# Turning image blocks on the vector engine: an edit of the first-image stages of a two-layer kernel

## The chip, the cores and the metric

The kernel runs on one core of a Trainium2 chip. The metric is device time in microseconds of one execution; lower is better. Before the change the median of three runs is 2614.22 us (2608.95 to 2623.82). All data are 32-bit floats.

## The reference, cut to what matters

The reference has two layers over an image of 256 x 256 pixels with 128 channels. The first is gated attention over rows. The second takes the channel axis as width: it sees 256 tokens, each an image of H = 256 by W = 128, and applies Fourier layers. The change touches the mixer at the end of the second layer:

```python
h0 = instance_norm(attn, norm2_w, norm2_b)
h1 = fno_layer(h0, mix_wr[0], mix_wi[0], ..., (H, W), norm=True, act=True)
h2 = fno_layer(h1, mix_wr[1], mix_wi[1], ..., (H, W), norm=True)
out = instance_norm(h2, mon_w, mon_b) + attn
```

Here `fno_layer` is a skip (a 4 x 4 mix of the tokens of a group), plus a spectral convolution that keeps 32 frequencies along H and 16 along W, then, in the first of the two, a gelu. So after the gelu of h1 the kernel needs its Fourier transform: first along w (16 complex frequencies, 32 real rows), then along h. It also needs the statistics of the second skip of h1, for the norm.

## The kernel before, in words

The tokens are worked on in two halves, `a` = 0 and 1, of 128 tokens each. A half is an array of 128 partitions (tokens) by 256 x 128 pixels, cut into 16 blocks of 16 rows h, so 2048 pixels to a block. The half in work lies in SBUF in the tile `blocks`, and `hb[b]` is block b. Of its 16 rows, `by_turn` makes four turns j of four rows each.

The stage in question is `first_images` (L1720 to L1852), which runs once for each half. For each block it does the following.

- `first_skip` (L1813) multiplies the block by the 4 x 4 mixes, as 16 tiles of 32 x 32 of the array, into four PSUM banks `ups`, one for each turn. The banks come from pool `psk`, which has four.
- `image` (L1386) adds the inverse transform of the modes (tile `gs`, loaded from `Gd1`) into the same banks.
- `gelu` (L1819) has ScalarE (ACT) read a bank and write the gelu into `hb[b]`: four instructions.
- `turn_back` (L1770) has TensorE (PE) transpose the 16 pieces of 128 x 128 of a block against the identity into four banks `htps` of pool `pst` (four banks as well). VectorE (DVE) copies them into `hT`, and in half 1 ACT copies the one of turn 0 (L1780, L1789). The copies of turns 1, 2 and 3 also exchange pieces of 32 or 64 tokens, since a turn holds its tokens in exchanged order.
- `along_w` (L1800) multiplies by `bfwd` (128 pixels of w by 32 rows) into one bank `psA`, four tiles of 128 x 32 at once. ACT copies it to `yA`, and GpSimd (POOL) issues the store into `Yd` in HBM (L1808); the very last of half 1 is issued by ACT.
- `second_skip` (L1793) multiplies the block by the mixes of the second layer into four banks `sps` of `pst`, and DVE takes their statistics (`bn_stats`, L1798). Only the statistics are kept.

The order is written out by hand (`manual_schedule`), for the compute engines and for the queue of SyncE (SP), which issues the loads. In pass b of the loop at L1827 the order in half 0 is: first skip of b, second skip of b-2, image of b, gelus 0 and 1, transform of b-2, gelus 2 and 3, turn of b-1. In half 1 the second skip comes first. So PE has transform and turn to do behind an image.

Beside it, half 0 prepares w, the sum that the output needs: `add_w` (L1747) has ACT scale the block (L1755), POOL add x1 (L1758) and issue the store to `wd` (L1759). This is done in halves of a block, for 21 of 32; the other 11 are done earlier. In half 1 the generator `output_0` (L2151) writes out half 0 in between: after the turn of a pass it multiplies a block's second skip and image into four banks `h2ps` of pool `psk` (L2135 to L2137), ACT empties two of them and DVE two (L2139 to L2144), and then DVE adds w twice (L2148) and POOL issues the stores (L2149).

After the stage, `second_modes` (L1882, half 0) or `LastModes` (L1961, half 1) loads `Yd` into `YT` and transforms along h. `ystat` (L1440) holds the statistics of y that `first_modes` (L1653) sums up.

Tiles of one tag rotate through a fixed number of buffers, so an instruction that writes a buffer waits for those that read what was in it. That holds for PSUM banks too: the fifth bank asked of `pst` is the first again.

Of the kernel before, what the change touches and what calls it, by code (L numbers as in the profile page):

```python
# [10 lines left out]
FP = mybir.dt.float32  # L11
# [7 lines left out]
P = 128  # L19
# [681 lines left out]
def layer1(tc, I, C, ident, x1d, upool, U, Q2, groups, out):  # L701
# [6 lines left out]
    nc = tc.nc  # L708
    NT, H, W = 256, 256, 128
    L = lambda n: I["L1_conv_" + n]  # L710
    with ExitStack() as ctx:
# [667 lines left out]
        def by_turn(t):  # L1379

            return t.rearrange("p (n j w) -> p j n w", j=4, w=W)

        def rows_of(ps):
            return ps.rearrange("p (n w) -> p n w", w=W)

# [51 lines left out]

        sp = sp3
        hstat = sp.tile([P, 64, 6], FP, name="hstat")
        ystat = sp.tile([P, 2, 64, 6], FP, name="ystat")  # L1440
# [59 lines left out]
        def y_blocks(a, psum, lo, hi, also=None):  # L1500

            tt = slice(a * P, (a + 1) * P)
            gs = {}

            def load(u):
                if (a, u) not in xts:
                    xts[a, u] = load_x1(a, u)
                if u % 2 == 0:
                    gs[u // 2] = xp.tile([P, 4, P], FP, tag="gs", name=f"gs_{a}_{u}", bufs=3)
                    load_modes(gs[u // 2], Gd0, u // 2, tt)  # L1510

            load(lo)
            load(lo + 1)
            yield 0.0
            for u in range(lo, hi):
                b, s = u // 2, u % 2
                if u + 2 < hi:
                    load(u + 2)
                xt = xts.pop((a, u))
                ps = [psum.pool.tile([P, 512], FP, tag=psum.tag, name=f"yps_{a}_{u}_{j}") for j in range(4)]  # L1520
                ps = [z[:, 0:256] for z in ps]
                for j in range(4):
                    for sc in range(2):
                        nc.tensor.matmul(  # L1524
                            rows_of(ps[j]), mpT[:, sc, tt], by_turn(xt[:, sc])[:, j],
                            start=(sc == 0), stop=False,
                        )
                    if j < 3:
                        yield 0.86
                image(ps, gs[b], bsy, range(2 * s, 2 * s + 2))  # L1530
                if a == 0:
                    yt = blocks[:, b, s * HB : (s + 1) * HB]
                else:
                    yt = xp.tile([P, HB], FP, tag="yt", name=f"yt_{u}")
                for j in range(4):
# [107 lines left out]
        def first_modes(a, wp, mk, psum, gts):  # L1643
# [9 lines left out]
            nc.vector.bn_aggr(h.col[:, 0:2], ystat[:, a].rearrange("p k s -> p (k s)"))  # L1653
# [66 lines left out]
        def first_images(a, wp, yp, psk, pst, first=None, modes=()):  # L1720
# [44 lines left out]
            if a == 0:  # L1765
                load_w(0)
                add_w(0)
            hTs = {}

            def turn_back(b):  # L1770

                turned = by_turn(hb[b])
                hT = hTs[b] = {}
                for j in (1, 2, 3, 0):
                    ps = pst.tile(f"htps_{a}_{b}_{j}")
                    for n in range(4):
                        nc.tensor.transpose(ps[:, n * P : (n + 1) * P], turned[:, j, n, :], ident)  # L1777
                    t = hT[j] = wp.tile([P, 512], FP, tag="hT", name=f"hT_{a}_{b}_{j}", bufs=4)
                    if j == 0:
                        (nc.scalar.copy if a else nc.vector.tensor_copy)(t, ps)  # L1780
                        continue
                    v = t.rearrange("p (n c d x) -> p n c d x", n=4, c=2, d=2)
                    if j == 1:
                        v = v[:, :, :, ::-1].rearrange("p n c d x -> p (n c) d x")
                    elif j == 2:
                        v = t.rearrange("p (n c x) -> p n c x", n=4, c=2)[:, :, ::-1]
                    else:
                        v = t.rearrange("p (n c x) -> p n c x", n=4, c=4)[:, :, ::-1]
                    nc.vector.tensor_copy(  # L1789
                        v, ps.rearrange("p (m c x) -> p m c x", m=v.shape[1], c=v.shape[2])  # L1790
                    )

            def second_skip(b):  # L1793

# [4 lines left out]

            def along_w(b):  # L1800

                hT = hTs.pop(b)
                psA = pst.tile(f"psA_{a}_{b}")
                for j in (1, 2, 3, 0):
                    nc.tensor.matmul(psA[32 * j : 32 * j + 32, :], bfwd, hT[j], start=True, stop=True)  # L1805
                yA = wp.tile([P, 512], FP, tag="yA", name=f"yA_{a}_{b}")
                nc.scalar.copy(yA, psA)
# [74 lines left out]
        def second_modes(a, wp, mk, psum, gts, yts):  # L1882
# [5 lines left out]
            def load(c, hcs=(0, 1)):  # L1888
# [2 lines left out]
                    YT[c] = yp.tile([P, 2, 2, 512], FP, tag=tag, name=f"YT_{a}_{c}", bufs=bufs)  # L1891
                for hc in hcs:
                    nc.sync.dma_start(
                        YT[c][:, hc],
                        h.Yd[P * hc : P * hc + P].rearrange("h (r f) t -> h r (f t)", r=2)[
                            :, :, 4 * c * P : 4 * (c + 1) * P
                        ],
                    )

            def forward(c):  # L1900
                ps = psum.tile(f"f1ps_{a}_{c}")
                for r in range(2):
                    for hc in range(2):
                        for k in range(2):
                            for f in range(4):
                                nc.tensor.matmul(
                                    ps[32 * f : 32 * f + 32, r * P : (r + 1) * P],
                                    efwd[:, hc, (2 if r else 1) if k else 0, :],
                                    YT[c][:, hc, 1 - r if k else r, f * P : (f + 1) * P],
                                    start=(hc == 0 and k == 0), stop=(hc == 1 and k == 1),  # L1910
                                )
                nc.vector.tensor_copy(F[:, c].rearrange("p r t -> p (r t)"), ps[:, 0:256])
# [48 lines left out]
        class LastModes:  # L1961
# [5 lines left out]
            def load(self):  # L1967

                tile = lambda tag, bufs, n, name: xp.tile([P, 2, n], FP, tag=tag, name=name, bufs=bufs)
                rows = halves[1].Yd.rearrange("h (r f) t -> h r (f t)", r=2)  # L1970
                self.low = [tile("xt", 3, 1024, f"YT0_{k}") for k in range(2)]
                for k in range(2):
                    nc.sync.dma_start(self.low[k], rows[0:P, :, 1024 * k : 1024 * k + 1024])
                self.high = [tile("yt", 2, 512, f"YT1_{k}") for k in range(2)] + [tile("xt", 3, 1024, "YT1_2")]
                at = (slice(0, 512), slice(512, 1024), slice(1024, 2048))
                for lo, hi in ((0, 96), (96, P)):
                    for t, c in zip(self.high, at):
                        nc.sync.dma_start(t[lo:hi], rows[P + lo : P + hi, :, c])

            def spectrum(self, c, hc, r, f):  # L1980
                if hc == 0:
                    t, c = self.low[c // 2], c % 2
                else:
                    t, c = self.high[min(c, 2)], c % 2 if c > 1 else 0
                return t[:, r, 512 * c + f * P : 512 * c + (f + 1) * P]

            def synth(self, c, banks, gt, engines):

# [307 lines left out]
def constants():  # L2296
    H, W = 256, 128
    N = H * W
# [159 lines left out]
```

## Time and profile before

| | us |
|---|---|
| median of three runs | 2614.22 |
| profiled execution | 2609.25 |
| its span on the core | 2607.5 |
| first images of half 0, about | 1957 to 2083 |
| first images of half 1, about | 2233 to 2410 |
| PE busy in 1955 to 2083 | 118.74 of 128 |
| PE busy in 2230 to 2410 | 161.80 of 180 |
| DVE busy in the same two | 82.33 and 126.94 |
| ACT busy in the same two | 74.39 and 86.49 |
| POOL busy in the same two | 79.15 and 27.45 |
| transfers in the same two | 269 and 343 GB/s |

The profiled execution took 2609.25 us, of which the span of the core's records is 2607.5; it is 5 us below the median. A line of the timeline has the start in us, the busy time, engine, source line, operation, output and inputs, the shape and, after x, how many instructions were merged; a bracket at its end has the idle time before them and who ended it. A matmul's busy time overlaps that of the next, so that the step from start to start is the better measure. One 32-bit multiplication shows as two matmul instructions.

### The profile page before, as it was taken

What the parts mean: (1) busy time and instruction counts of PE and PEld (TensorE: products, weight loads), DVE (VectorE), ACT (ScalarE), POOL (GpSimd) and SP (SyncE); (2) the same over time, 40 slices, a digit from 0 to 9 for tenths busy, and PEclk for the clock granted to TensorE, in tenths of its full rate; (3) what the DMA queues carried; (4) which work ended last, traced back from release to release, by engine and by line L of the source; (5) the groups of instructions that cost most, each with busy time, mean ns of one, the idle gap of its engine ahead of it and who ended that gap; (6) DMA issues with size and microseconds to landing.
All of it is one profiled execution on the core that took longest, in us unless ns stands there. A gap on an engine that the chain in (4) does not pass through costs nothing. (4 is left out here: it accounts for less than half of the span.)

```text
span 2607.5 us, 88724 instructions
## 1 busy us (share of the span) xinstructions
PE 2393.2 (92%) x37598; PEld 1557.0 (60%) x37598; DVE 2051.0 (79%) x2908; ACT 1399.1 (54%) x2700; POOL 1474.4 (57%) x1043
## 2 busy tenths in 40 slices
PE   7799999999999999999999999998989988799754
PEld 6555656566556565665655667787675566455533
DVE  7799999999999999999998547566656655577455
ACT  0377888888888888888887222100016401344232
POOL 1299999999999999999997003001136511111011
PEclk9999999999999999999999999999999998899855
DMA  9755566666566565565663110788898774999599
GB/s 364 222 101 104 102 108 105 105 107 105 104 108 106 104 106 104 106 107 102 109 105 71 23 59 16 258 274 260 310 336 279 251 242 138 334 365 318 190 382 345
DMA packets 1016549, 458.49 MB, mean 176 GB/s; under 512 B 831062, under 2 KB 946729, under 8 KB 1009752
## 3 DMA queue, kind: packets, MB, share of 16 engines
q1 hardware_dynamic: 980120, 364.71, 55.5%
q0 software_dynamic: 22832, 81.54, 8.1%
q10 hardware_dynamic: 13200, 6.56, 0.9%
q8 instruction: 298, 4.88, 0.8%
q14 instruction: 99, 0.81, 0.1%
HBM read 317.36 MB, written 135.27 MB: 174 GB/s over the span
## 5 line engine op out<-in xcount | busy, mean ns | idle before, releaser
L422 POOL TENSOR_TENSOR e<-e,b1T 128x1024 f32<-128x1024 f32 x255 | 604.5, 2370 | 83.3 <-ACT e L404 82.7
L427 POOL TENSOR_TENSOR es<-e 128x512 f32<-128x512 f32 x512 | 648.0, 1288 | 0.1
L449 DVE RECIPROCAL av<-av 128x256 f32<-128x256 f32 x256 | 452.2, 1766 | 9.1
L404 ACT ACTIVATE sc<-sc,b2T 128x512 f32<-128x512 f32 x514 | 339.9, 662 | 123.1 <-PE sc L395 110.9
L404 ACT ACTIVATE e<-sc,b2T 128x512 f32<-128x512 f32 x510 | 322.9, 693 | 0.0
L420 DVE TENSOR_TENSOR e<-sc,b1T 128x1024 f32<-128x1024 f32 x257 | 312.2, 1215 | 6.7 <-ACT sc L404 3.5
L395 PE MATMUL sc<-qkT 32*128 32x256 f32 x4096 | 294.4, 401 | 1.8 <-DVE e L420 1.8
L437 PE MATMUL av<-e,v 128*32 128x256 f32 x4096 | 268.6, 379 | 1.8 <-DVE gate L450 1.7
L1524 PE MATMUL yps<-xt,mpT 128*128 128x256 f32 x1024 | 246.7, 391 | 22.3 <-DVE yt L1536 15.1
L395 PEld LDWEIGHTS sc<-qkT 32*128 32x128 f32 x4096 | 185.7, 184 | 113.7 <-issue 52.3
L1524 PEld LDWEIGHTS yps<-xt,mpT 128*128 128x128 f32 x1024 | 192.0, 193 | 67.5 <-DVE yt L1536 20.4
L437 PEld LDWEIGHTS av<-e,v 128*32 128x32 f32 x4096 | 130.1, 109 | 125.9 <-issue 38.5
L1540 POOL DMA_DIRECT2D yd<-yt x32 | 17.4, 544 | 320.1 <-DVE yt L1536 315.4
L2149 POOL DMA_DIRECT2D out_dram<-w x64 | 34.2, 534 | 258.9 <-DVE w L2148 258.2
L367 ACT ACTIVATE qkT<-qk,qb 128x512 f32<-128x512 f32 x256 | 174.0, 680 | 3.1 <-PE qk L337 3.0
L337 PE MATMUL qk<-turned,wT_wk 128*32 128x256 f32 x2048 | 163.9, 392 | 0.8 <-DVE g_ve L35 0.8
L494 ACT ACTIVATE turned<-turned 128x256 f32<-128x256 f32 x256 | 104.3, 408 | 112.2 <-DVE x1b L462 109.8
L337 PEld LDWEIGHTS u<-adft,x 128*32 128x32 f32 x4096 | 118.4, 110 | 74.9 <-issue 74.7
L442 PE MATMUL av<-es,ones 128*32 128x256 f32 x2048 | 160.7, 379 | 1.6 <-POOL es L427 1.6
L345 DVE STREAM_TRANSPOSE turned<-xk 128x1024 f32<-128x1024 f32 x128 | 158.1, 1235 | 0.4 <-DMA xk<-in_L_conv_kv_x_dram 0.4
L337 PE MATMUL qk<-turned,wn_wq 128*32 128x256 f32 x2048 | 157.9, 380 | 0.0
L1822 ACT ACTIVATE blocks<-ups,turn 128x512 f32<-128x512 f32 x128 | 92.5, 781 | 89.0 <-PE ups L1391 55.8
(575 smaller groups left out, 4277.1 us busy)
## 6 DMA issues: line engine op xcount, KB each, us to landing
xt<-x1d SPq DMA_DIRECT2D x128, 512.0 KB, 8.1
U<-in_x_dram SPq DMA_DIRECT2D x32, 1024.0 KB, 10.3
xk<-in_x_dram SPq DMA_DIRECT2D x512, 64.0 KB, 3.2
xk<-in_L_conv_kv_x_dram SPq DMA_DIRECT2D x512, 64.0 KB, 2.7
x1d<-x1b SPq DMA_DIRECT2D x512, 64.0 KB, 2.2
out_dram<-w POOLq DMA_DIRECT2D x64, 512.0 KB, 7.8
x<-x1d SPq DMA_DIRECT2D x126, 256.0 KB, 3.2
y<-yd SPq DMA_DIRECT2D x62, 512.0 KB, 8.8
```

The costliest lines, as they stand in the source:

```text
L337: nc.tensor.matmul(out[hd], w[:, hd], src, start=start, stop=stop)
L345: nc.vector.transpose(turned[:, a : b + 1 : b - a].rearrange("p k (b c) -> p k b c", c=32), t)
L367: nc.scalar.activation(r["qkT"], ps, AF.Identity, bias=self.qb)
L395: nc.tensor.matmul(sc[h // 2][:, h % 2, c * 256 : (c + 1) * 256], qkT[p, 256 + c * P : 256 + (c + 1) * P], qkT[p, 0:256], start=True, stop ...
L404: nc.scalar.activation(r["e"][1][:, :, c, :] if hp and s < NS - 1 else z, z, AF.Exp, bias=b2T[:, c, s : s + 1])
L420: nc.vector.tensor_tensor(e, sc.rearrange("p h x -> p (h x)"), w, ALU.mult)
L422: nc.gpsimd.tensor_tensor(e, e, w, ALU.mult)
L427: nc.gpsimd.tensor_tensor(es, e[:, :, 0, :], e[:, :, 1, :], ALU.add)
L437: nc.tensor.matmul(ps[hd, 0:256], p["v"][:, 2 * (s % 2) + c, hd], r["e"][h // 2][:, h % 2, c, :], start=(c == 0), stop=(c == 1),)
L442: nc.tensor.matmul(ps[32 * h : 32 * h + 32, 256:512], self.ones, r["es"][h // 2][:, h % 2, :], start=True, stop=True,)
L449: nc.vector.reciprocal(rd, rd)
L1524: nc.tensor.matmul(rows_of(ps[j]), mpT[:, sc, tt], by_turn(xt[:, sc])[:, j], start=(sc == 0), stop=False,)
```

## The change

`turn_back` no longer uses PE. Two DVE instructions transpose a block in pieces of 32 x 32, straight from `hb[b]` into one tile `hT` of 128 x 2048. After that, a partition is a group of 32 tokens (four of them) and a w within a quarter; the group index stays on the partitions. `along_w` therefore multiplies with block-diagonal weights of 64 x 64 (two groups, each 32 w of a quarter by 32 rows), accumulates over the four quarters of w, and does so for two halves of the partitions (r) and two sets of rows h (j): 16 multiplications of 256 columns, into two banks `psA`. The weights have the token exchange in them. ACT copies each bank's 128 x 256 into `yA`. `Yd` gets another order, in which a store writes runs of 64 tokens, and the readers follow it. The order in a pass is now the same in both halves: transform of b-2, second skip of b-2, first skip of b, image of b, four gelus, turn of b-1. `hT` has one buffer in place of four quarter ones. `ystat` is shared by the halves.

```diff
-            h.Yd = dram.tile([H, 32, P], FP, name=f"Yd_{a}")
+            h.Yd = dram.tile([H, 2, 2, 16, 64], FP, name=f"Yd_{a}")
...
-                    nc.vector.bn_stats(ystat[:, a, 2 * u + g, :], yt[:, g * 512 : (g + 1) * 512])
+                    nc.vector.bn_stats(ystat[:, 2 * u + g, :], yt[:, g * 512 : (g + 1) * 512])
...
             def turn_back(b):
-                turned = by_turn(hb[b])
-                hT = hTs[b] = {}
-                for j in (1, 2, 3, 0):
-                    ps = pst.tile(f"htps_{a}_{b}_{j}")
-                    for n in range(4):
-                        nc.tensor.transpose(ps[:, n * P : (n + 1) * P], turned[:, j, n, :], ident)
-                    t = hT[j] = wp.tile([P, 512], FP, tag="hT", name=f"hT_{a}_{b}_{j}", bufs=4)
...
+                T = turned[b] = wp.tile([P, 8, 8, 32], FP, tag="hT", name=f"hT_{a}_{b}", bufs=1)
+                src = hb[b].rearrange("p (n k l x) -> p k n l x", k=2, l=8, x=32)
+                for k in range(2):
+                    nc.vector.transpose(T[:, :, k::2].rearrange("p l n x -> p n l x"), src[:, k])
...
             def along_w(b):
-                hT = hTs.pop(b)
-                psA = pst.tile(f"psA_{a}_{b}")
-                for j in (1, 2, 3, 0):
-                    nc.tensor.matmul(psA[32 * j : 32 * j + 32, :], bfwd, hT[j], start=True, stop=True)
-                yA = wp.tile([P, 512], FP, tag="yA", name=f"yA_{a}_{b}")
-                nc.scalar.copy(yA, psA)
+                T = turned.pop(b)
+                ps = [pst.tile(f"psA_{a}_{b}_{r}") for r in range(2)]
+                for c in range(4):
+                    for j in range(2):
+                        for r in range(2):
+                            q, o = slice(64 * r, 64 * r + 64), slice(64 * j, 64 * j + 64)
+                            nc.tensor.matmul(
+                                ps[r][o, 0:256], bfwd[q, j, c], T[q, 4 * j + c],
+                                start=(c == 0), stop=(c == 3),
+                            )
+                yA = wp.tile([P, 4, 4, 32], FP, tag="yA", name=f"yA_{a}_{b}")
+                for r in range(2):
+                    nc.scalar.copy(
+                        yA[:, :, 1:3] if r else yA[:, :, 0::3],
+                        ps[r][:, 0:256].rearrange("p (n k x) -> p n k x", k=2, x=32),
+                    )
                 (nc.scalar if a and b == 15 else nc.gpsimd).dma_start(
-                    h.Yd[16 * b : 16 * b + 16].rearrange("(n j) f t -> (j f) n t", j=4),
-                    yA.rearrange("f (n t) -> f n t", n=4),
+                    h.Yd.rearrange("(k l) r g f x -> (l r g f) k x", l=2)[:, 8 * b : 8 * b + 8],
+                    yA.rearrange("p n (k h) x -> p (n k) (h x)", k=2),
                 )
...
-                if a and 1 < b < 17:
+                if b > 1:
+                    along_w(b - 2)
+                if 1 < b < 17:
                     second_skip(b - 2)
                 if b < 16:
                     ps = first_skip(b)
-                if not a and 1 < b < 17:
-                    second_skip(b - 2)
-                if b < 16:
                     image(ps, gss.pop(b), bs4)
-                    gelu(b, ps, (0, 1))
-                if b > 1:
-                    along_w(b - 2)
-                if b < 16:
-                    gelu(b, ps, (2, 3))
+                    gelu(b, ps, range(4))
                 if 0 < b < 17:
                     turn_back(b - 1)
...
-    c["bfwd"] = bw.reshape(32, W).T / N
+    fw = np.zeros((2, 2, 32, 2, 4, 2, 2, 16))
+    for g in range(2):
+        for j in range(2):
+            fw[:, g, :, j, :, :, g ^ j] = (bw.reshape(2, 16, 4, 32) / N).transpose(3, 2, 0, 1)
+    c["bfwd"] = fw.reshape(128, 2, 4, 64)
```

The readers of `Yd` load rows of four frequencies of 64 tokens (1 KB) where they loaded 2 KB, or 2 KB where they loaded 4 KB, and the multiplications along h read their moving operand in runs of 32 tokens (`by_token`).

More of the change, by code (lines that the diff above doesn't have):

```diff
@@ L1381, in by_turn, with by_token @@
             return t.rearrange("p (n j w) -> p j n w", j=4, w=W)
+        def by_token(t):
+            return t.rearrange("p (g f h x) -> p f h g x", g=2, h=2, x=32)
         def rows_of(ps):
@@ L1439, in layer1 @@
         hstat = sp.tile([P, 64, 6], FP, name="hstat")
-        ystat = sp.tile([P, 2, 64, 6], FP, name="ystat")
+        ystat = sp.tile([P, 64, 6], FP, name="ystat")
         with tc.tile_pool(name="psb", bufs=4, space=PSUM) as psa:
@@ L1652, in first_modes @@
             ym, yv, ra, lam, r2, rho, sig = (h.col[:, k : k + 1] for k in range(7))
-            nc.vector.bn_aggr(h.col[:, 0:2], ystat[:, a].rearrange("p k s -> p (k s)"))
+            nc.vector.bn_aggr(h.col[:, 0:2], ystat.rearrange("p k s -> p (k s)"))
             yield 1.0
@@ L1767, in first_images @@
                 add_w(0)
-            hTs = {}
+            turned = {}
             def turn_back(b):
-                turned = by_turn(hb[b])
-                hT = hTs[b] = {}
-                for j in (1, 2, 3, 0):
-                    ps = pst.tile(f"htps_{a}_{b}_{j}")
-                    for n in range(4):
-                        nc.tensor.transpose(ps[:, n * P : (n + 1) * P], turned[:, j, n, :], ident)
-                    t = hT[j] = wp.tile([P, 512], FP, tag="hT", name=f"hT_{a}_{b}_{j}", bufs=4)
[L1779 to L1791, printed above, removed]
+                T = turned[b] = wp.tile([P, 8, 8, 32], FP, tag="hT", name=f"hT_{a}_{b}", bufs=1)
+                src = hb[b].rearrange("p (n k l x) -> p k n l x", k=2, l=8, x=32)
+                for k in range(2):
+                    nc.vector.transpose(T[:, :, k::2].rearrange("p l n x -> p n l x"), src[:, k])
             def second_skip(b):
@@ L1893, in load @@
                     nc.sync.dma_start(
[L1894 to L1897, printed above, removed]
+                        YT[c][:, hc].rearrange("p r (g f x) -> p r g f x", g=2, x=64),
+                        h.Yd[P * hc : P * hc + P, :, :, 4 * c : 4 * c + 4],
                     )
@@ L1908, in forward @@
                                     efwd[:, hc, (2 if r else 1) if k else 0, :],
-                                    YT[c][:, hc, 1 - r if k else r, f * P : (f + 1) * P],
+                                    by_token(YT[c][:, hc, 1 - r if k else r])[:, f],
                                     start=(hc == 0 and k == 0), stop=(hc == 1 and k == 1),
@@ L1969, in load @@
                 tile = lambda tag, bufs, n, name: xp.tile([P, 2, n], FP, tag=tag, name=name, bufs=bufs)
-                rows = halves[1].Yd.rearrange("h (r f) t -> h r (f t)", r=2)
+                rows = halves[1].Yd
+                part = lambda t: t.rearrange("p r (g f x) -> p r g f x", g=2, x=64)
                 self.low = [tile("xt", 3, 1024, f"YT0_{k}") for k in range(2)]
                 for k in range(2):
-                    nc.sync.dma_start(self.low[k], rows[0:P, :, 1024 * k : 1024 * k + 1024])
+                    nc.sync.dma_start(part(self.low[k]), rows[0:P, :, :, 8 * k : 8 * k + 8])
                 self.high = [tile("yt", 2, 512, f"YT1_{k}") for k in range(2)] + [tile("xt", 3, 1024, "YT1_2")]
-                at = (slice(0, 512), slice(512, 1024), slice(1024, 2048))
+                at = (slice(0, 4), slice(4, 8), slice(8, 16))
                 for lo, hi in ((0, 96), (96, P)):
                     for t, c in zip(self.high, at):
-                        nc.sync.dma_start(t[lo:hi], rows[P + lo : P + hi, :, c])
+                        nc.sync.dma_start(part(t[lo:hi]), rows[P + lo : P + hi, :, :, c])
             def spectrum(self, c, hc, r, f):
@@ L1984, in spectrum @@
                     t, c = self.high[min(c, 2)], c % 2 if c > 1 else 0
-                return t[:, r, 512 * c + f * P : 512 * c + (f + 1) * P]
+                return by_token(t[:, r])[:, 4 * c + f]
             def synth(self, c, banks, gt, engines):
```

## The prediction

> **What bounds the kernel now.** The page first: PE is busy 92% of the span, but that is a mean over stages, and the change touches two of them, the first images of half 0 (about 1957 to 2083 us) and of half 1 (about 2233 to 2410 us). The window table for these gives PE 118.7 of 128 us and 161.8 of 180 us at a granted clock of 0.97 and 0.96, so PE sets the pace in both; in the second the transfers run at 343 GB/s with a DMA share of 0.98. Then the timelines, one engine at a time. Half 0, one block, PE:
>
> ```profile
> 1982.43 1.17 PE L1391 MATMUL ups<-k_bsyn,gs 32*128 32x128 f32 x32
> 1983.54 1.06 PE L1805 MATMUL psA<-hT,k_bfwd 128*32 128x512 f32 x8
> 1984.53 1.97 PE L1777 MATMUL htps<-ident,blocks 128*128 128x128 f32 x16
> 1986.43 1.22 PE L1406 MATMUL ups<-blocks,bl 32*32 32x512 f32 x28
> ```
>
> From start to start: image 1.11, transform 0.99, turn 1.90, and the two skips 2.66 to the next image at 1989.09: 6.66 us per block with no gap. ACT and DVE beside it:
>
> ```profile
> 1983.68 1.45 ACT L1822 ACTIVATE blocks<-ups,turn 128x512 f32<-128x512 f32 x2 [1.32 <-PE ups L1391]
> 1985.02 0.58 ACT L1807 COPY yA<-psA 128x512 f32<-128x512 f32 x1
> 1985.49 1.47 ACT L1822 ACTIVATE blocks<-ups,turn 128x512 f32<-128x512 f32 x2
> 1986.83 2.20 ACT L1755 ACTIVATE w<-blocks,col 128x1024 f32<-128x1024 f32 x2
> ...
> 1985.23 1.89 DVE L1789 COPY hT<-htps 128x512 f32<-128x512 f32 x3 [0.78 <-PE htps L1777]
> 1987.03 0.68 DVE L1780 COPY hT<-htps 128x512 f32<-128x512 f32 x1
> 1988.62 2.49 DVE L1798 BATCH_NORM_STATS2 hstat<-sps 128x6 f32<-128x512 f32 x4 [0.91 <-PE sps L1406]
> ```
>
> The reader is to see that the first gelu starts 1.25 us after the image, that yA is copied between two pairs of gelus, and that transform and turn (2.89 us of PE) fill the time in which ACT empties the four image banks. Half 1, one block, is the same with the output of half 0 in between:
>
> ```profile
> 2290.09 1.17 PE L1391 MATMUL ups<-k_bsyn,gs 32*128 32x128 f32 x32
> 2291.93 1.06 PE L1805 MATMUL psA<-hT,k_bfwd 128*32 128x512 f32 x8 [0.66 <-DVE hstat L1798]
> 2292.93 1.97 PE L1777 MATMUL htps<-ident,blocks 128*128 128x128 f32 x16
> 2294.82 1.29 PE L1406 MATMUL h2ps<-blocks,bl 32*32 32x512 f32 x32
> 2296.04 1.17 PE L1391 MATMUL h2ps<-k_bsyn,gs 32*128 32x128 f32 x32
> ```
>
> One block is 10.03 us here; from image 0 (2236.34) to image 15 (2394.75) the mean is 10.56, since y and mode loads hold PE for 1 to 2 us in every second block.
>
> **The change, part by part.** PE loses the turn (1.90) and the old transform (0.99) of each block. It gains 16 multiplications of 64x64 weights by 256 columns. The image multiplies 16 times by 128 columns, four tiles of the array at a time, in 1.11 us; twice the columns, again four tiles, is **2.0 us**; the synthesis at 2434.79 confirms the rate (32 times 128 columns in 2.0). From below, 32 instructions do not pass in under the image's 1.1; from above, two tiles at a time make 4.0. I take 2.0, since image and synthesis also change weights each time. PE's own work falls by 0.9 us per block.
>
> DVE loses four copies per block in half 0 and three in half 1, 0.605 us apart, and gains two transposes of 128x1024. L345 has 1.235 us for one; pieces of 32 elements cost no more, since L1789's reversed copies take 678 to 692 ns whatever their pieces. So 2.4 us: even in half 0, +0.5 in half 1, where DVE has some 8.9 of 10 us to do. ACT copies yA in two pieces of 128x256: between the 0.41 of L494 and half of 0.58, I take 0.40 each; in half 1 it loses its 0.59 copy.
>
> The order is what costs. The changed program's order has, on ACT, the yA copies of block b-2 ahead of the gelus of block b, and so behind the gelus **and the two w scalings** of block b-1. And the four banks of the second pool now rotate as two for psA and four for sps, so that sps 2 and sps 3 take over the banks that yA has just read: both wait for ACT. Behind sps 2 on PE stand the first skip and the image of the next block, for which ACT's gelus wait in turn: a closed loop. The transposes stand on DVE behind four bn_stats, and psA behind them.
>
> *Half 0, blocks with two w scalings.* From an image's start: gelus from 1.25, four of them 0.67 apart, 3.93; two w, 6.03; two yA, 6.83; release 0.1 and the last quarter of sps 0.29, 7.22; first skip 1.16: the next image starts at **8.4**, where it was 6.66. PE stands meanwhile: about 1.1 us ahead of the transform (the transposes are queued on DVE behind four bn_stats, and the transform waits for them) and 1.7 between sps 1 and sps 2. The 21 additions on POOL fall in blocks 2 (one), 3 to 8 and 12 to 15, which makes ten such steps: 84. Three steps without w are bounded by DVE: transform 2.0, sps 0 0.39, four bn_stats 2.42, two transposes 2.34, signal 0.1, is 7.25: 21.8. The first two steps are 5.0 (as now) and 7.3. Image 0 to image 15 is then 118 where the trace has 104.0 (2061.98 less 1957.99; it has about 5 us of waits for modes, which the longer period hides): **+14**.
>
> *End of half 0.* Now 20.2 us pass from image 15 to the last sps, 12.2 of them in ACT's waits for the store of Yd, whose issues stand behind additions on POOL. With 8.4 us per block POOL (2 x (2.37 + 0.30 + 0.57) + 1.07 = 7.55) keeps up. The way is then: gelus to 3.9, yA of block 14 to 5.0, sps 5.5, bn_stats 6.2, transposes 8.6, transform 10.7, yA 11.5, sps 12.2. That is 8 less; I keep 2 for stores that land late: **-6**. (1.07 for Yd's issue: 0.53 for 128 pieces, 0.76 for 512, the same slope to 1024.)
>
> *Half 1.* From the image's start: gelus end at 4.0, and now nothing stands between the image and h2ps, whose four banks wait for one gelu each; last bank 4.1 to 4.4; second image 5.5; transform 7.5; sps with yA 8.8; skip of y 2.07: **10.87** where 10.03 was the undisturbed step. If the load waits stay, 14 x 0.84 = +12; if the longer step hides them all, 14 x (10.87 - 10.56) = +4. **+8**. After the last image the transposes of block 15 wait behind the bn_stats of block 14, and there are two yA copies: **+3**, on the path to the modes.
>
> *Yd.* A store has 1024 pieces of 256 B for 512 of 512 B. Bounds: nothing, and the same 256 KB once more at the 379 GB/s that the last stage moves (2470 to 2590), 0.7 us. Half 1 moves 3.9 MB a block, 10.4 us at that rate, and 11.1 with it: **+1**. The loads of YT in 1 KB rows I cost at nothing: Gd stores around 1630 us, all in packets of 0.5 to 2 KB, run at about 340 GB/s. The shared ystat and the constant cost nothing.
>
> *The clock.* After 1.44 us of idle PE the timeline has
>
> ```profile
> 2013.49 2.26 PE L1391 MATMUL ups<-k_bsyn,gs 32*128 32x128 f32 x32 [1.44 <-DMA gs<-Gd]
> 2015.68 1.94 PE L1805 MATMUL psA<-hT,k_bfwd 128*32 128x512 f32 x8
> ```
>
> and the window table (busy time of PE, weight loads, DVE, ACT, POOL, then the granted clock, DMA share, GB/s)
>
> ```profile
> 2016.00:2018.00 2.00, 2.00 (x10) 0.46 (x3) 0.00 (x0) 1.20 (x3) 1.00 (x1) 0.50 0.99 316
> ```
>
> a clock of 0.50 and 2.2 us lost (image 1.1, transform 0.9, turn 0.2 over their usual 1.17, 1.06 and 1.97), while pauses of 1.18, 1.56 and 1.98 us passed without. The changed order pauses PE for 1.1 and 1.7 (half 0) and 2.0 (half 1) in some 27 blocks; at nothing to 2.2 each, I take **+4** of 0 to 59, as few pauses did it. The Trainium skill ("TensorE: Matmul & The Clock Gate", section "Why this matters for your kernels") lets pauses pass up to about 3 us; by it this term would be nothing and the sum 4 us lower, and the row above speaks against it.
>
> Sum: 14 - 6 + 8 + 3 + 1 + 4 = **+24 us**. On the profiled execution (2609.25, span 2607.5) that is 2633; the median of the runs is 5 us above it, so **2638**.
>
> **Rivals.**
>
> *PE's saved work is the gain* (faster). 32 x 0.9 = 28 us less: 2586. For it: both stages are PE's. Against: it needs ACT to reach yA before PE needs its banks, and the order puts 4.8 us of gelus and w ahead. 0.07.
>
> *Transfers set the pace, and the slack is taken up* (no change). Half 1 is then +4, half 0 as little as +8, its end -8, the rest +1: about 2619. For it: the DMA share of 0.98. Against: half 0 averages 277 GB/s (1965 to 2070), against 379 in the last stage, so its longer steps hide behind nothing. 0.16.
>
> *Slow multiplications* (slower than forecast). Tiles of 64x64 that overlap only in part, 3 us instead of 2, add 14 in half 1 and 4 in half 0, 2656; or the clock falls in half of the blocks, +30. Decided from 2.5 us upwards. 0.17.
>
> **Numbers.** Forecast 0.60. 2638 is the likeliest. Low end 2612 (the second rival, and the transform near 1.1 us), high end 2678 (3.5 us, or the clock in most blocks). What tells from no change here is 0.5%, 13 us. Slower by more than that: all but a little of the forecast and all of the third rival, 0.76; same 0.17; faster 0.07.
>
> **What would show it.** The step of half 0 near 8.4 where w is scaled and 7.2 where not; sps waiting for yA, h2ps for gelus, psA for the transposes; L1796 16 multiplications in 2.0; the transposes 1.24; no ACT wait for Yd's stores at the end of half 0. Wrong if the steps stay at 6.7 and 10.0, if the transform needs far from 2 us, or if the loss sits in transfers.

## The result and the profile after

The changed kernel takes 2645.39 us (median of four runs, 2641.80 to 2653.54), the kernel before beside it 2612.70 (2608.95 to 2623.82): a ratio of 1.0111, with a 95% interval of 1.0084 to 1.0139. The profiled execution after took 2647.55 us, with a span of 2645.8. A run's ratio is to runs of the kernel before made with it, and leaves out disturbed runs, so it can differ a little from a quotient of two medians.

Three measures, read from PE's timeline, serve for all runs below: the **loop of half 0** (start of image 0 to start of image 15), the **loop of half 1** (the same), and the **stretch** from image 0 of half 0 to the first matmul into `z1acc` behind half 1. The last holds both stages, and some 150 to 160 us between the halves, in which the change alters only how `Yd` is read, and which differ by up to 8 us from profile to profile.

| us | before | after | difference |
|---|---|---|---|
| image 0 of half 0 starts at | 1958.0 | 1964.4 | +6.4 |
| loop of half 0 | 104.0 | 129.6 | +25.6 |
| image 15 to the last sps of half 0 | 20.3 | 15.4 | -4.9 |
| from there to image 0 of half 1 | 154.1 | 152.6 | -1.5 |
| loop of half 1 | 158.4 | 171.9 | +13.5 |
| image 15 to z1acc | 30.3 | 27.9 | -2.4 |
| z1acc to the end | 182.4 | 184.0 | +1.6 |
| stretch | 467.1 | 497.4 | +30.3 |

The first row lies ahead of the edited stages: the spans differ by 38.3 us, of which I do not count these 6.4 to the change, since among the runs below that share the changed kernel's code up to there image 0 starts anywhere from 1958.5 to 1974.4. The medians differ by 32.7, near the stretch's 30.3.

One pass of half 0 with two w scalings, PE, ACT and DVE of the changed kernel:

```profile
2015.11 1.17 PE L1395 MATMUL ups<-k_bsyn,gs 32*128 32x128 f32 x32
2017.60 1.96 PE L1796 MATMUL psA<-hT,k_bfwd 64*64 64x256 f32 x32 [1.31 <-DVE hT L1779]
2019.49 1.09 PE L1410 MATMUL sps<-blocks,blk 32*32 32x512 f32 x16
2021.53 0.91 PE L1410 MATMUL sps<-blocks,blk 32*32 32x512 f32 x8 [0.96 <-ACT yA L1802]
2021.84 0.66 PE L1410 MATMUL ups<-blocks,bl 32*32 32x512 f32 x8
2021.99 0.88 PE L1410 MATMUL sps<-blocks,blk 32*32 32x512 f32 x8
2022.29 1.66 PE L1410 MATMUL ups<-blocks,bl 32*32 32x512 f32 x24
2023.88 1.18 PE L1395 MATMUL ups<-k_bsyn,gs 32*128 32x128 f32 x32
...
2016.36 2.78 ACT L1820 ACTIVATE blocks<-ups,turn 128x512 f32<-128x512 f32 x4 [3.38 <-PE ups L1395]
2019.03 2.19 ACT L1759 ACTIVATE w<-blocks,col 128x1024 f32<-128x1024 f32 x2
2021.10 0.65 ACT L1802 COPY yA<-psA 128x256 f32<-128x256 f32 x2
...
2022.66 1.30 DVE L1786 BATCH_NORM_STATS2 hstat<-sps 128x6 f32<-128x512 f32 x2 [0.75 <-PE sps L1410]
2023.88 2.35 DVE L1779 STREAM_TRANSPOSE hT<-blocks 128x1024 f32<-128x1024 f32 x2
```

From image to image 8.77 us. PE stands twice: ahead of the transform, which waits for the transposes, and between sps 1 and sps 2, which wait for yA, which stands on ACT behind four gelus and two scalings. The transposes stand behind the statistics of the late sps, and the next transform behind them.

One pass of half 1, PE of the changed kernel:

```profile
2319.77 1.77 PE L1395 MATMUL ups<-k_bsyn,gs 32*128 32x128 f32 x32
2321.84 3.07 PE L1410 MATMUL h2ps<-blocks,bl 32*32 32x512 f32 x32 [0.30 <-ACT blocks L1820]
2324.84 1.17 PE L1395 MATMUL h2ps<-k_bsyn,gs 32*128 32x128 f32 x32
2325.94 1.96 PE L1796 MATMUL psA<-hT,k_bfwd 64*64 64x256 f32 x32
...
2330.97 1.17 PE L1395 MATMUL ups<-k_bsyn,gs 32*128 32x128 f32 x32
```

The skip into h2ps shows 3.07 us where it had 1.29: it is spread out by its wait for the gelus. The step is 11.20.

The windows of the two loops (busy time of PE, weight loads, DVE, ACT, POOL; granted clock, DMA share, GB/s), before and then after:

```profile
1958.00:2062.00 104.00, 100.15 (x1739) 59.71 (x1737) 69.06 (x113) 69.95 (x94) 67.10 (x52) 0.98 0.79 266
2236.00:2395.00 159.00, 143.67 (x3127) 85.23 (x3124) 111.64 (x151) 78.06 (x116) 24.65 (x41) 0.98 1.00 354
```

```profile
1964.00:2094.00 130.00, 97.49 (x1878) 52.58 (x1860) 69.39 (x90) 71.67 (x109) 74.19 (x57) 0.95 0.69 232
2262.00:2434.00 172.00, 152.31 (x3238) 80.69 (x3238) 118.77 (x139) 72.34 (x117) 27.44 (x43) 0.97 0.98 333
```

In half 0 PE is busy 97 of 130 us, where before it was 100 of 104. The time went into standing.

### The profile page after: what moved, and what is told of

Same layout as the page of the kernel before. It is cut to its first block, busy times and chain, and to the rows that moved or that the text cites. A ratio compares the mean times of both kernels' runs of the same rounds, so it can differ in the third digit from the quotient of the medians.

```text
span 2645.8 us, 89148 instructions
## 1 busy us (share of the span) xinstructions
PE 2392.8 (90%) x37854; PEld 1543.0 (58%) x37854; DVE 2050.6 (78%) x2860; ACT 1389.3 (53%) x2716; POOL 1477.9 (56%) x1043
## 5 line engine op out<-in xcount | busy, mean ns | idle before, releaser
L337 PE MATMUL qk<-turned,wT_wk 128*32 128x256 f32 x2048 | 164.1, 392 | 0.4 <-DVE g_ve L35 0.4
```

The costliest lines, as they stand in the source:

```text
L337: nc.tensor.matmul(out[hd], w[:, hd], src, start=start, stop=stop)
```

## The experiments

The theory behind the forecast: the loss comes from the new pass order, which lines up waits in a closed loop, and from the lost cover, since TensorE's turn had filled the time in which ACT empties the image banks. The main rival: the new parts cost it themselves (DVE's transposes, 64x64 multiplications, two evictions, 256-byte pieces).

**1. The new parts in the old order** (`old_order`).

```diff
-                if b > 1:
-                    along_w(b - 2)
-                if 1 < b < 17:
+                if a and 1 < b < 17:
                     second_skip(b - 2)
...
-                    gelu(b, ps, range(4))
+                    gelu(b, ps, (0, 1))
+                if b > 1:
+                    along_w(b - 2)
+                if b < 16:
+                    gelu(b, ps, (2, 3))
```

> The changed kernel (DVE turn, 64x64 transform, Yd in 256-byte pieces) with the pass order of before: skips, image, gelus 0 and 1, transform, gelus 2 and 3, turn. Theory 'order' (the loss comes from putting the transform at the head of the pass, where it waits for DVE's turn and, in half 0, for ACT behind the w scalings, with nothing left on PE to cover it): the half-0 loop from image 0 to image 15 falls from 129.6 us to 103-112, half 1 from 171.9 to 150-162, the time to 2600-2620, at or below before's 2612.7. Rival 'parts' (the DVE transposes, the 16 small matmuls, the two evictions or the 256-byte pieces cost it themselves, wherever they stand): the loops stay near 125 and 170 us and the time at 2635-2650.

Measured: 2628.39 us, ratio to before 1.0033 (1.0010 to 1.0056); loops 110.6 and 167.6, stretch 478.2. The loop of half 0 is where the theory put it; half 1 is nearer to the rival's 170, and the time lies between the two ranges.

**2. The old parts in the new order** (`order_only`): the kernel before with only the loop body of the change.

```diff
-                if a and 1 < b < 17:
+                if b > 1:
+                    along_w(b - 2)
+                if 1 < b < 17:
                     second_skip(b - 2)
                 if b < 16:
                     ps = first_skip(b)
-                if not a and 1 < b < 17:
-                    second_skip(b - 2)
-                if b < 16:
                     image(ps, gss.pop(b), bs4)
-                    gelu(b, ps, (0, 1))
-                if b > 1:
-                    along_w(b - 2)
-                if b < 16:
-                    gelu(b, ps, (2, 3))
+                    gelu(b, ps, range(4))
```

> The kernel before (TensorE turn, 32-row transform, long Yd runs) with nothing changed but the pass order, which is the changed kernel's. Theory 'order': half 0 from 104.0 us to 115-128 for the loop, because the transform now waits at the head of the pass for DVE's copies and ACT's yA behind the w scalings; half 1 from 158.4 to 160-172; time 2625-2650. Rival 'parts': the order is nothing, 2608-2618.

Measured: 2631.58 us, ratio 1.0036 (1.0013 to 1.0059); loops 125.2 and 161.8, stretch 486.1. Half 0, PE of this kernel:

```profile
2016.79 1.17 PE L1391 MATMUL ups<-k_bsyn,gs 32*128 32x128 f32 x32
2017.89 1.97 PE L1777 MATMUL htps<-ident,blocks 128*128 128x128 f32 x16
2019.79 2.38 PE L1805 MATMUL psA<-hT,k_bfwd 128*32 128x512 f32 x8
2022.10 1.11 PE L1406 MATMUL sps<-blocks,blk 32*32 32x512 f32 x24
2023.42 0.63 PE L1406 MATMUL sps<-blocks,blk 32*32 32x512 f32 x4 [0.21 <-ACT yA L1807]
```

With the turn still on TensorE the step is 8.71, almost the changed kernel's 8.77: psA directly behind the turn waits for DVE's copies within its 2.38 us (1.06 before), and sps for yA.

The two runs and the two kernels make a table of four. In the stretch the new order adds 19.0, the new parts 11.1, both together 30.3, near their sum. In the loop of half 0 the order is 21.2 and the parts 6.6 (together 25.6); in half 1 it is the other way round, 3.4 and 9.2 (together 13.5). In the undisturbed steps the two overlap: in half 0 6.66 before, 8.71 with the order, 7.24 with the parts, 8.77 with both; in half 1 about 10.1, 10.5, 11.55 and 11.2. In the runs 0.36% and 0.33% stand beside 1.11%, each with some 0.2 to 0.3 to either side, so the medians do not settle whether the two add up. For half 0 the theory holds in its first part alone: the order costs as much with the turn still on PE, so no lost cover is needed there. In half 1 something of the new parts is most of it; and there order_only has about 1 us more to do on PE per pass than the changed kernel and is yet 0.65 us faster. The lost cover explains that: behind the turn its h2ps passes in 1.56 us without a pause (at 2302.19), where the changed kernel's takes 3.07.

**3. Which of the new parts** (`short_transform`): old_order with two quarters of w left out of the transform's sum.

```diff
-                for c in range(4):
+                for c in range(2):
...
-                                start=(c == 0), stop=(c == 3),
+                                start=(c == 0), stop=(c == 1),
```

> old_order with half of the transform's matmuls (two of the four quarters of w are left out of the sum, so the output is not the reference's): psA takes about 1.0-1.1 us instead of 1.96, as long as the 32-row transform of before. DVE's turn, both evictions and the 256-byte pieces stay. Theory 'cover': the 0.9 us longer transform is what the new turn costs in the old order; half-0 step 7.24 to 6.6-6.8, half 1 steps 11.55 to 10.4-10.7, time 2612-2620. Rival (the other parts cost it): steps within 0.2 us of old_order, time 2625-2631.

Measured: 2611.76 us, ratio 0.9987 (0.9971 to 1.0004): no difference from before. Loops 107.3 and 159.3, stretch 470.2; the half-0 step 6.71 and that of half 1 10.7 in its quiet passes, as expected. So in this order the loss that shows in the time comes with the 0.9 us longer transform. DVE's turn, the evictions and the small pieces are not shown to be free by this: PE has 1.9 us less to do per pass than before and the step of half 0 is the same, so waits have taken the place of the turn, and the quiet passes of half 1 are still some 0.6 us above those of before. Where the transform acts is seen in half 1 of old_order, PE and then ACT:

```profile
2323.09 2.55 PE L1796 MATMUL psA<-hT,k_bfwd 64*64 64x256 f32 x32 [0.66 <-DVE hstat L1786]
2325.57 1.09 PE L1410 MATMUL h2ps<-blocks,bl 32*32 32x512 f32 x16
2327.06 1.73 PE L1410 MATMUL h2ps<-blocks,bl 32*32 32x512 f32 x16 [0.40 <-ACT blocks L1820]
...
2325.68 0.65 ACT L1802 COPY yA<-psA 128x256 f32<-128x256 f32 x2 [1.73 <-PE psA L1796]
2326.21 1.46 ACT L1820 ACTIVATE blocks<-ups,turn 128x512 f32<-128x512 f32 x2
```

Gelus 2 and 3 wait behind yA, yA waits for the longer transform, and the last two h2ps banks wait for the gelus. Before, 1.97 us of transposes on PE lay between. The transform shows 2.55 us here and not 1.96, since it starts behind DVE's statistics and, by the times, its second bank waits for the next of them.

**4. All gelus ahead of yA, in the old order** (`gelus_first`): in old_order `gelu(b, ps, range(4))` directly behind the image, then `along_w`.

> The changed kernel with the pass order of before, but all four gelus of a block ahead of the two yA copies on ACT; PE's order is that of the run old_order (transform right after the image). Theory 'cover' (with the old order the new turn costs because the transform is 0.9 us longer and gelus 2 and 3 wait on ACT behind yA, which waits for it; TensorE's transposes of 1.9 us had filled just that time): PE's wait for gelus goes, the half-0 step falls from 7.24 to 6.5-6.9 (then POOL's adds and stores of w, 6.5-7.3 us, set it), half 1 from 11.5 to 9.9-10.6 (PE needs about 9.3, the transfers then set it); from image 0 of half 0 to the spectrum of half 1 455-470 us where before took 467.1 and old_order 478.2; time 2603-2622. Rival: the new turn costs by something else (DVE, two evictions, Yd's pieces) and old_order's 2628 stays.

Measured: 2616.03 us, ratio 0.9998 (0.9982 to 1.0015); loops 104.8 and 164.1, stretch 477.8 (the profiled execution, 2622.7 us of span, is above this kernel's median). The whole loss is gone, with DVE's turn, the evictions, the small pieces and the full transform all in place, and no gain is left. The waits in its loop of half 0 (us in total, times, longest) and the window of half 1 say what has come up from below:

```profile
PEld ups L1395 <- DMA gs<-Gd: 10.6, 13, 2.0
...
PE ups L1395 <- DMA gs<-Gd: 5.3, 10, 1.2
```

```profile
2246.00:2410.00 164.00, 140.94 (x3203) 78.23 (x3200) 116.90 (x136) 71.63 (x115) 26.40 (x41) 0.93 0.99 342
```

Undisturbed passes of half 0 take 6.17 (6.66 before), but five in the middle take 7.5 to 9.1, since the image waits for its modes; in half 1 the transfers are busy for 0.99.

**5. Lighter transfers in half 1** (`gelus_light` from gelus_first, `after_light` from the changed kernel): the second y load of a block is left out from block 1 on, and the first piece is used twice.

```diff
-                    for k in (2 * b, 2 * b + 1):
+                    for k in (2 * b, 2 * b):
+                        if ys[b]:
+                            ys[b].append(ys[b][0])
+                            continue
```

> gelus_first with one of the two y loads of each block of half 1 left out from block 1 on (the first piece is used twice, so the output is not the reference's): 0.5 MB less a pass. Theory 'transfers set half 1 of gelus_first': steps from 10-14 us to 9.2-9.8, the loop of half 1 from 164 to 140-150, time 2592-2605. Rival (PE with its waits sets it): the loop stays within 5 us of 160.

> The changed kernel with the same y loads left out (the output is not the reference's). Theory: there the chain image, gelus, h2ps, its image, transform, skips sets the step of 11.16 us, whatever the transfers do: steps of 11.1-11.2 throughout, the loop falls only by its few longer steps, from 171.9 to 166-169, time 2638-2645. Rival (transfers): the loop falls to 160 or below.

Measured: gelus_light 2608.80, ratio 0.9967 (0.9946 to 0.9988), loop of half 1 152.8; after_light 2650.77, ratio 1.0146 (1.0110 to 1.0182), loop of half 1 168.5 with steps of 11.16 to 11.21 nearly throughout. The changed kernel's half 1 is thus set by its chain on PE and ACT, not by transfers; its total lies above what I expected, but not apart from the changed kernel's interval. In gelus_first the transfers do set a part: 11 us by the two loops, some 8 us by the two ratios, as gelus_first's profile was one of its longer runs. The 140 to 150 were too low: passes with a pause still have slow transforms (3.2 and 3.6 us), so what else holds that loop stays open.

**6. The Yd pieces** (`yd_long`): the store in runs of 2 KB (the readers keep the changed kernel's order).

```diff
-                    h.Yd.rearrange("(k l) r g f x -> (l r g f) k x", l=2)[:, 8 * b : 8 * b + 8],
-                    yA.rearrange("p n (k h) x -> p (n k) (h x)", k=2),
+                    h.Yd[16 * b : 16 * b + 16].rearrange("k r g (u f) x -> (k r g u) (f x)", f=8),
+                    yA.rearrange("p n k x -> p (n k x)"),
```

> The changed kernel with each block's Yd store written in runs of 2 KB to the same bytes, in an order that the readers do not expect (the output is not the reference's); everything else as it is. If the 256-byte pieces are free: loops 129.6 and 171.9 us within 2 us, time 2642-2650. If they load the transfers, half 1 (DMA share 0.95) gains 4 us or more and the step falls below 11.0: 2636-2641.

Measured: 2648.30, ratio 1.0118 (1.0092 to 1.0145); loops 130.8 and 170.7. The pieces cost nothing that shows: the median from issue to landing is 7.2 us after, 7.0 in yd_long and 7.0 before. Only POOL's issue differs, 0.91 to 0.55 us.

**7. The w scalings** (`w_late`): in half 0 the scaling of block b stands behind the yA of pass b instead of ahead of it, and the w loads move with it.

```diff
-                    if a == 0:
-                        load_w(b + 1)
                 if b > 1:
                     along_w(b - 2)
+                if a == 0 and 0 < b < 16:
+                    add_w(b)
+                if a == 0 and b < 15:
+                    load_w(b + 1)
...
-                if a == 0 and b < 15:
-                    add_w(b + 1)
```

> The changed kernel with the scalings of w for block b moved on ACT behind the two yA copies of pass b (still ahead of gelu(b)), with the w loads one step later on SP. Theory 'order', its half-0 part (yA waits on ACT behind the two w scalings, so PE waits for yA before sps 2 and 3, and first for gelus that end later): the w step of half 0 falls from 8.77 to 7.2-7.7 us, the loop by 10-18 us, half 1 is unchanged, time 2627-2636. If instead PE in that loop is bound by DVE's turn and statistics, the step stays at 8.6-8.8 and the time at 2642-2650.

Measured: 2652.71, ratio 1.0119 (1.0066 to 1.0171); the loop of half 0 129.7. A miss: behind the first two, some steps are 8.0 to 8.4 and the others 9.1 to 9.6, and the sum is that of the changed kernel. Two passes of this kernel, PE, and two windows:

```profile
2033.31 1.96 PE L1796 MATMUL psA<-hT,k_bfwd 64*64 64x256 f32 x32 [2.07 <-DVE hT L1779]
...
2041.23 2.55 PE L1796 MATMUL psA<-hT,k_bfwd 64*64 64x256 f32 x32 [1.98 <-DVE hT L1779]
```

```profile
2033.00:2035.00 2.00, 1.69 (x32) 1.33 (x32) 0.16 (x1) 1.10 (x2) 2.00 (x1) 1.00 0.80 320
...
2043.00:2045.00 2.00, 2.00 (x32) 0.65 (x33) 0.00 (x0) 0.65 (x2) 0.82 (x2) 0.50 0.58 222
```

The wait for yA is gone, but the transform now waits about 2 us (1.9 to 2.4) for DVE in nearly every pass, and in about every second one the granted clock falls to 0.50. Two runs test that.

**8. PE kept busy** (`filler` from the changed kernel, `w_late_filler` from w_late, there in half 0 only).

```diff
+                for k in range(6 if b < 15 else 0):
+                    nc.tensor.matmul(ps[0][:, 256:320], ident, ident[:, 0:64], start=True, stop=True)
```

> The changed kernel with six extra 128x128x64 matmuls into columns of the psA bank that nobody reads, ahead of each transform, so that PE works while it would wait for the transposes (1.3 us a pass; 2 to 2.8 in the passes whose transform took 2.8-3.5 us instead of 1.96). The result is unchanged. Theory 'clock' (those transforms are slow because PE has just stood still): slow transforms become rare, each pass that had one gains 0.5-1.5 us, and the mean granted clock in half 0 rises from 0.94 towards 0.97; time 2635-2645. If the clock has nothing to do with the pause: slow transforms stay, and the extra matmuls add 0-1 us a pass, 2645-2665.

> w_late with six extra 128x128x64 matmuls into columns that nobody reads ahead of each transform of half 0 alone. In w_late the step was 7.9-8.1 us in the passes with a 1.96 us transform and 9.2 in those with 2.6-2.8 us, at a granted clock of 0.89; PE stood still for 2 us in each. Theory 'clock': with that pause filled every pass takes 7.9-8.0, the loop of half 0 falls from 129.7 to 116-121 us, the clock there rises to 0.97-1.0, half 1 stays at 170-172, time 2630-2640. If the pause is not what lowers the clock: loop 126-132, time 2645-2660.

Measured: filler 2657.84, ratio 1.0133 (1.0091 to 1.0175), loops 127.1 and 184.3; w_late_filler 2626.52, ratio 1.0048 (1.0031 to 1.0066), loops 117.9 and 170.6. The windows of the half-0 loop, w_late and then w_late_filler:

```profile
1970.00:2100.00 130.00, 97.80 (x1878) 55.49 (x1867) 68.01 (x88) 72.68 (x109) 73.09 (x56) 0.89 0.69 225
```

```profile
1961.00:2079.00 118.00, 110.24 (x2040) 69.47 (x2024) 67.73 (x88) 72.47 (x109) 72.57 (x56) 0.99 0.75 244
```

In w_late_filler nearly every pass takes 7.83: extra work on PE made the loop 11.8 us shorter, and of the 25.6 us that half 0 had lost, 11.7 are back. (The medians of the two differ by 26 us, more than that: in the profiles some 9 of it lie ahead of image 0, where the two kernels are the same.) In the changed kernel itself the filler gives 2.5 us in half 0. Its total is a miss, since in half 1 the same six matmuls lie on the path: every step there grows from 11.16 to 12.64, by the 1.48 that they take. That alone shows that PE's chain sets half 1.

**9. A version that might beat both.** From gelus_first: in `gelus_split` DVE adds the second w piece of a block in half 0, and in `gelus_act` ACT issues Yd's stores of half 0.

```diff
-                    nc.gpsimd.tensor_tensor(t[:, px], t[:, px], ys.pop((b, s)), ALU.add)
+                    (nc.vector if s and b else nc.gpsimd).tensor_tensor(t[:, px], t[:, px], ys.pop((b, s)), ALU.add)
```

```diff
-                (nc.scalar if a and b == 15 else nc.gpsimd).dma_start(
+                (nc.scalar if not a or b == 15 else nc.gpsimd).dma_start(
```

> gelus_first with the second of a block's two additions of w in half 0 on DVE instead of POOL (DVE has 4.8 us of work in a step of 6.17). In gelus_first half 0 kept the 6.17 step only until POOL, which needs 2.37+0.30+0.57 twice and 0.91 for Yd's issue (7.4 us a step), fell behind and held the xw buffers and with them SP's queue: steps of 7.5 to 9.1 us. Theory (POOL is the next limit there): those steps fall to 6.2-7.2 and the half-0 loop from 104.8 to 94-100; half 1, which the transfers set, stays at 157-165; time 2604-2615, so at best 0.4% faster than before. Rival (the transfers already set half 0 as well): the loop stays at 103-106 and the time at 2612-2620.

> gelus_first with Yd's store of half 0 issued by ACT right behind the two yA copies instead of by POOL. POOL then needs 6.5 us a step instead of 7.4, ACT 2.79+0.65+0.9+2.2 = 6.5 instead of 5.65, PE 6.17. Theory (POOL, through the xw buffers and SP's queue, is what stretched the middle steps of gelus_first to 7.5-9.1): half-0 loop from 104.8 to 97-102, time 2606-2615. Rival (the transfers, not POOL's time, hold xw and gs there): the loop stays at 103-107 and the time at 2612-2620.

Measured: gelus_split 2643.92, ratio 1.0105 (1.0073 to 1.0137), loop of half 0 135.0: a miss, as DVE's addition takes twice its time beside POOL's and the statistics stand behind it (below). The clock is a part of that loss too, since the granted clock in this loop is 0.86 (0.95 in gelus_first): in the middle passes the transform, 1.96 us at full clock, comes out twice as long:

```profile
1998.20 4.16 PE L1796 MATMUL psA<-hT,k_bfwd 64*64 64x256 f32 x32 [2.66 <-DVE hstat L1786]
```

gelus_act 2613.76, ratio 0.9977 (0.9956 to 0.9998): it beats the changed kernel. Against the kernel before it is 0.2% lower, with an interval that just clears 1; as the best of several variants, that is no shown gain. Its half-0 loop did not shrink (107.2 against 104.8), though POOL had less to do. But that does not clear POOL: the image's waits for its modes are nearly gone there (2.8 us of its weight loads' time in the loop, for 10.6), and PE waits for ACT's gelus instead (10.1 us for 1.7). ACT itself now stands for 17.6 us ahead of its w scalings, where Yd's stores are issued, and in gelus_first not at all. One wait took the place of another, and what stretches the middle passes of gelus_first was not separated.

## Why the prediction was right, and where its sizes were off

The forecast was +24 us, by the order and the lost cover. The medians give +32.7. The four-way comparison bears the order out for half 0, and the lost cover, with the longer transform, for half 1. That the total came this near has some luck in it: the two loops lost 39 us where the terms for them (14, 8, 1 and 4) came to 27, and the tail, forecast at +3, gave 2.4 back.

- **The w step of half 0**, 8.4: measured 8.77. Up to ACT it held (gelus from 1.25, w at 3.92, yA at 5.99 after the image). The step that failed is the last: "the last quarter of sps 0.29" and first skip 1.16 behind the release. The prediction had itself said that sps 2 and sps 3 both wait for yA, but its sum has one quarter behind it. Both came after yA, beside the whole first skip, 2.35 us from sps 2 to the image for my 1.45; the release after the first of the two yA gave part of that back.
- **The passes without w**, three of 7.25: 7.26, 9.18 and 9.57, and with the filler 7.37, 7.88 and 7.83. The chain was right to 0.1 to 0.6 us, and the clock took most of the rest. All in all the loop is +25.6 for my +14.
- **The end of half 0**, -6: measured -4.9, with ACT's 12.2 us of waits for Yd's stores gone.
- **Half 1**, +8: measured +13.5. The step is 11.16 to 11.2 for 10.87. The term that was too small is the last h2ps bank: in the pass at 2319.77 the second image starts 5.07 us after the first for my 4.4, and the transform and the skips behind it gave 0.3 back. Fourteen steps that are some 1.15 longer make 16, so the longer step hid 2 to 3 us of load waits: the upper of the two cases, and a little more. The filler and after_light show that the chain sets it.
- **The tail**, +3: measured -2.4. The wait that I had named is there, as the last transform stands 4.17 us for its transposes. But I had not counted that PE's 4.0 us wait at `f1ps`, which the trace of before puts down to YT and Yd, would go. The transfers are busy for 0.31 of the 12 us behind the last store of Yd, where it was 0.60; that this is why was not tested.
- **The Yd pieces**, +1: nothing that shows (experiment 6).
- **The transform**, 2.0: 1.96 with the clock up. The transposes, 1.235: 1.20 to 1.25. yA, 0.40: 0.65 for the two. The third rival, a transform of 3 us, falls.
- **The clock**, +4: the direction was right. Half 0 alone holds 2.5 of it by the filler. In w_late the same effect ate a gain of 11.8. The pauses of half 1 brought next to none: its loop has a granted clock of 0.97 for 0.98 before.
- **The first rival**, PE's saved work as a gain: gelus_first lets it through in its undisturbed passes (6.17 for 6.66), and waits for loads and transfers take it.

The Trainium skill ("TensorE: Matmul & The Clock Gate", section "Why this matters for your kernels") lets PE pause for up to about 3 us. Here, in w_late, seven of the eight falls of the clock to 0.50 follow single pauses of 1.9 to 2.4 us, which come once a pass, and filling them brought the clock back: the measurement decides.

## What to carry to other kernels

Work on the bound engine can be a cover for a wait: taking it away shows a gain only if the wait behind it goes too, so look at what ends the pause once the work is gone. When an edit moves an engine's work and the order of a pass at once, run the two apart; here they had different culprits in different stages. Put a copy that waits for a long producer behind the work that others await (gelus_first). Putting a copy that frees a bank ahead of long work on its engine that nobody awaits paid here only once PE's pause was filled as well (w_late and w_late_filler).

## What was not expected of the hardware

In these loops of half 0 the granted clock falls in pieces of 3.4 us at 0.50. There is one such piece before, four after, eight in w_late, one in w_late_filler and none in order_only, where PE never stands for long.

DVE's addition beside POOL's, in half 0 of gelus_split, and DVE's of the same shape in half 1, where POOL adds nothing:

```profile
L1762 DVE TENSOR_TENSOR w<-w,xw x11: 1225/2504/3822, 1976.0 to 2097.3; 128x1024 f32<-128x1024 f32 x11
```

```profile
L2143 DVE TENSOR_TENSOR w<-w,blocks x26: 1217/1222/1226, 2255.7 to 2400.0; 128x1024 f32<-128x1024 f32 x26
```

The three figures are the least, the median and the longest in ns. In the middle pass one looks as follows:

```profile
2005.16 2.57 DVE L1762 TENSOR_TENSOR w<-w,xw 128x1024 f32<-128x1024 f32 x1 [0.35 <-ACT w L1759]
```

```profile
2004.27 2.37 POOL L1762 TENSOR_TENSOR w<-w,xw 128x1024 f32<-128x1024 f32 x1
```

DVE's ends at 2007.73, 1.09 us after POOL's, which is near the 1.22 us that it takes alone, as if it had waited for POOL and then run. The Trainium skill ("SBUF — State Buffer", section "Who interferes with whom") says that a DVE instruction with two inputs in SBUF and a GpSimd one that reads SBUF shut each other out, and this agrees.
